# A graph-attention layer on one NeuronCore: batch 1's row flags by ScalarE, its x loaded later, value blocks cleared earlier

## The chip, the core and the metric

The kernel runs on one core of a Trainium2 chip. A core has a matrix engine (TensorE, PE in the profile, with PEld for its weight loads), VectorE (DVE), ScalarE (ACT), GpSimd (POOL), a queue processor for transfers (SyncE, SP) and 16 DMA engines between the chip's memory and the core's own (SBUF; PSUM receives the matrix products). Each engine works through its own instructions in order and waits on semaphores for the others. The metric is the device time of one execution in microseconds; lower is better.

## The reference

The layer gets x (16 batches, 512 nodes, 512 features), a condition vector per batch, and an integer adjacency (16, 512, 512, 11). Cut to what matters:

```python
row_zero = v.sum(-1) == 0                      # one flag for each node
q_exp = where(row_zero[..., None], 0.0, q[:, None, :])
self_feat = concat([v, q_exp], -1) @ W_self.T + b_self
output = self_feat
for d in range(2):                             # adjacency, and its transpose
    A = (adj if d == 0 else swap(adj))[:, :, :20, :]
    mask = A.sum(-1) > 0;  vb = A @ w_bias + b_bias
    kv = self_feat[:, :20]                     # 20 neighbours
    aff = (self_feat @ Wq[d].T + bq[d]) . (kv @ Wk[d].T + bk[d]) / sqrt(32)   # 16 heads
    w = softmax(where(mask, aff, -9e15) + vb)
    output += (w @ kv) @ Wout[d] + bout[d]     # by head
return v + relu(output)
```

A node whose features sum to zero gets no condition term. That flag for each node (the "row flag") is what the change computes in another way for batch 1.

## The kernel before

Everything is float32. There is a setup for all 16 batches together, and then a loop over the batches, in each of which four tiles of 128 nodes go through scores, softmax and weighted sum. The order of the instructions is written out by hand; no scheduler changes it. Tile pools decide which buffers are shared.

**Setup.** The 20 neighbours of all batches (320 columns) go through the self-feature product, the key product (`key_rows`) and, with Wq folded in, into keys ready for scores. `keys(runs)` works these out in 22 bursts of three half-batches each: matmuls into two PSUM pairs, then an eviction by ScalarE (one pair, L575) and VectorE (the other, L577) into a staging tile `st`, of which there are four. A staging tile is complete after four halves and goes out on SyncE's queue: the keys of batch 0 into `g0` (L582; the last four are copied by GpSimd, L584), those of batch 1 into the array `g1_d` (L585), those of batches 2 to 15 into `g_d` (L586, 1120 KB). Behind each burst stands filler work of TensorE, by `plan`: one word for each burst, one letter for each step ("b" biases, "c" bias scores, "v" and "w" values, "s" one step of batch 0's self features, "n" row flags of a batch). Extra work of other engines is hung on burst numbers (`if n == 10` and so on).

**Row flags.** For batches 0 and 1 GpSimd adds the four feature chunks of the transposed x (`row_sums`, three additions), and TensorE sums over the partitions with a matrix of ones (`row_flags`, L172), which also puts the sums on all partitions; VectorE compares with zero (L174). For batches 2 to 15 ScalarE sums rows of x in its natural layout (`row_sum`, L152, four passes for a batch on the tile `xn`), VectorE compares (`row_mask`, L156), SyncE stores 2 KB into `nz_d` (L157) and later loads it back on all partitions (`load_nz`, L161).

**Value blocks.** `blocks` puts projected values from `vw_d` into a block layout `bd_d` in memory (12 transfers, L145). What it doesn't write must be zero: `clear_blocks` writes zeros there for all batches (6 transfers, L129). `load_values` reads a batch's blocks (4 transfers, L117).

**The loop.** For batch b and tile nt, TensorE does the self-feature parts that `ahead` names (`self_feat`, L189), in tiles 0 and 1 the second half of batch b's nodes, in tile 3 the first half of batch b+1's, and then `scores` (L254). So batch 1's x is first read in tile 3 of batch 0. The weighted sums (`attend`, L321) of the batch before come in tile 2. VectorE evicts (`self_copy`, L202, which uses the row flags; `weigh`, L265 to L269), ScalarE takes exponentials, GpSimd normalises and adds masks. Transfers stand at fixed tiles: in tile 1 the next batch's adjacency half and `cq`, in tile 2 the value loads, keys, x two batches ahead and the other adjacency half. All of these go out on SyncE's queue in program order, and a transfer that has to wait holds those behind it.

Of the kernel before, what the change touches and what calls it, by code (L numbers as in the profile page):

```python
# [18 lines left out]
def gat_kernel(  # L19
# [53 lines left out]
    zero = const.tile([32, P], F32, name="zero")  # L73
# [12 lines left out]
    def load_x(b):  # L86
        xs[b] = load.tile([P, C, N], F32, tag="x", name=f"x{b}", bufs=4)
        nc.sync.dma_start(xs[b], xT[b].rearrange("(c p) n -> p c n", p=P))
# [74 lines left out]
    def row_sums(b):  # L163

        t = rss[b] = load.tile([P, 2, F], F32, tag="xn", name=f"rx{b}")[:, 0]
        nc.gpsimd.tensor_add(t, xs[b][:, 0], xs[b][:, 1])
        for k in range(2, C):
            nc.gpsimd.tensor_add(t, t, xs[b][:, k])
# [65 lines left out]
    def full_add(b, nt):  # L234
        f = fulls[b, nt] = msk.tile([P, H * S], F32, tag="full", name=f"full{b}_{nt}").rearrange(
            "p (g h m) -> p g h m", g=2, m=S
        )
        shape = [P, 2, H // 2, S]
        nc.gpsimd.tensor_add(  # L239
            f, cqs[b].unsqueeze(1).to_broadcast(shape),  # L240
            adds[b, nt // 2][:, nt % 2].unsqueeze(2).to_broadcast(shape),
        )
# [109 lines left out]
    with tc.tile_pool(name="setup", bufs=1) as sp:  # L352
# [18 lines left out]
        with tc.tile_pool(name="setup_k", bufs=1) as sk:  # L371
# [46 lines left out]
            nc.sync.dma_start(bo_sb, bout)  # L418
            for d in range(2):
                rows(wo_sb[:, d], woT[d])  # L420
            load_x(1)
            load_adj(0, 1)


# [80 lines left out]
        with tc.tile_pool(name="setup_g", bufs=4) as sg:  # L505
# [82 lines left out]
            def self_step(b, f, h, i, k):  # L588
# [5 lines left out]
            steps = {  # L594
                "b": [(biases, ())],
                "c": [(bias_scores, (d,)) for d in range(2)],
                "n": [(row_flags, (b,)) for b in range(2)],
                "s": [
                    (self_step, (0, f, h, i, k)) for f, h in ((0, 0), (1, 0), (0, 1))
                    for i in range(2) for k in range(C)  # L600
# [1 line left out]
                "v": [(values, (t, (d,), k)) for t in range(2) for d in range(2) for k in range(C)],  # L602
                "w": [(values, (2, (0, 1), k)) for k in range(C)],
            }
            plan = "bvv vv vv ccw vv ns ssss sssw vv vv ssss ssss vv vv nww ssss ssss".split()

            halves = [(fc, hg, d, i) for fc in range(C) for hg in range(C) for d in range(2) for i in range(2)]
            bursts = []
# [10 lines left out]
            for n, runs in enumerate(bursts):  # L619
                for i in range(len(rest)):  # L620
                    if i < (4 if n == 0 else 1) or any(fc == 0 and (d, hg) == rest[0] for fc, hg, d, _, _ in runs):
                        key_rows(*rest.pop(0))
                keys(runs)
                if rest:
                    for d in range(2):
                        bias_terms(d, n)
                    continue
                first = n if first is None else first
                for kind in plan[n - first] if n - first < len(plan) else ():
                    f, args = steps[kind].pop(0)  # L630
                    f(*args)
                if n == 7:
                    mask_count(0, 0)
                if n == 8:
                    mask_mul(0, 0)
                if n == 10:
                    mask_add(0, 0)
                    load_cq(0)
                if n == 11:
                    row_sums(1)  # L640
                if n == 12:
                    mask_count(0, 1)
                if n == 14:
                    mask_mul(0, 1)
                if n == 18:
                    full_add(0, 0)

    soft = ctx.enter_context(tc.tile_pool(name="soft", bufs=2))
    gp = ctx.enter_context(tc.tile_pool(name="gp", bufs=2))
# [2 lines left out]

    gs[0] = g0
    with tc.manual_schedule():
        load_keys(1)

        def side(t, lo, hi, q):

# [15 lines left out]
        for b in range(B):  # L674
# [13 lines left out]
            for nt in range(NT):  # L688
                store()
                if nt == 1:  # L690
                    if b + 1 < B:
                        load_adj(b + 1, 0)
                        load_cq(b + 1)
                    if b == 0:
                        clear_blocks(zero)
                        blocks()
                if nt == 2:
                    load_values(b)
# [78 lines left out]
                if nt < NT - 1:  # L777
                    if (b, nt + 1) not in fulls:
                        full_add(b, nt + 1)
                    if b == B - 1 and nt < 2:  # L780
                        ns = slice(nt * (N - P), N)
# [15 lines left out]
        b = B - 1  # L797
# [83 lines left out]
```

## Time and profile before

| | |
|---|---|
| three runs | 630.17, 630.88, 630.75 us (median 630.75) |
| the profiled execution | 630.1 us, of which the span in the trace is 627.1 us |
| granted TensorE clock | 1.00 |
| TensorE busy | 619.6 us |
| VectorE, GpSimd, ScalarE busy | 506.2, 342.1, 217.9 us |
| setup until batch 0's first scores | 91.65 us |
| one batch in the loop | some 33.3 us |

Timeline rows give the start and duration in us, the engine, the line, output<-input, how many instructions are merged, and in brackets the idle time before them and what ended it. "SPq" is SyncE issuing a transfer; its duration is that of the issue, not of the transfer. In rows by stretches each engine has its busy time and instruction count, in the order PE, PEld, DVE, ACT, POOL; the last three columns are the granted clock, the mean share in which the DMA engines were busy (packets overlap, so that it can be above 1), and GB/s.

### The profile page before, as it was taken

What the parts mean: (1) busy time and instruction counts of PE and PEld (TensorE: products, weight loads), DVE (VectorE), ACT (ScalarE), POOL (GpSimd) and SP (SyncE); (2) the same over time, 40 slices, a digit from 0 to 9 for tenths busy, and PEclk for the clock granted to TensorE, in tenths of its full rate; (3) what the DMA queues carried; (4) which work ended last, traced back from release to release, by engine and by line L of the source; (5) the groups of instructions that cost most, each with busy time, mean ns of one, the idle gap of its engine ahead of it and who ended that gap; (6) DMA issues with size and microseconds to landing.
All of it is one profiled execution on the core that took longest, in us unless ns stands there. A gap on an engine that the chain in (4) does not pass through costs nothing.

```text
span 627.1 us, 16412 instructions
## 1 busy us (share of the span) xinstructions
PE 619.6 (99%) x6830; PEld 380.3 (61%) x6830; DVE 506.2 (81%) x809; ACT 217.9 (35%) x480; POOL 342.1 (55%) x268
## 2 busy tenths in 40 slices
PE   8999999999999999999999999999999999999997
PEld 6654558866565656565565656565656565655654
DVE  1377657789888888888888979798888888888896
ACT  1445422133242424241524334332424242415341
POOL 2406332537556474738292847465564747382974
PEclk9999999999999999999999999999999999999999
DMA  8999998629284655738391919393757657492513
GB/s 303 399 393 320 360 389 247 219 76 304 102 251 154 188 219 120 286 97 310 56 350 33 334 45 290 112 289 116 232 174 186 220 135 271 87 320 49 184 36 135
DMA packets 88976, 131.53 MB, mean 210 GB/s; under 512 B 8808, under 2 KB 59016, under 8 KB 86856
## 3 DMA queue, kind: packets, MB, share of 16 engines
q1 hardware_dynamic: 87656, 128.61, 61.8%
q0 software_dynamic: 672, 1.36, 0.9%
q8 instruction: 53, 0.87, 0.6%
q10 hardware_dynamic: 576, 0.53, 0.3%
q14 instruction: 19, 0.16, 0.1%
HBM read 90.89 MB, written 39.92 MB: 209 GB/s over the span
## 4 chain that ended last, share of the span: by engine, by line
PE 97%; DMA 1%; issue 0%; SPq 0%; DVE 0%; ACT 0%; DVEq 0%
PE ps_s L254 44%; PE ps_sf L189 34%; PE ps_o L321 7%; PE ps_v L533 3%; PE ps_k L480 3%; DMA ws_q<-in_wsT 1%; PE ps_kv L431 1%; PE ps_o L667 1%; PE ps_nz L172 0%; PE ps_c L511 0%; PE ps_g(0, 3, 0, 0, 2)0_367 L560 0%; PE ps_q L441 0%; PE ps_g(1, 3, 1, 0, 2)0_530 L560 0%; PE ps_g(1, 1, 0, 1, 2)0_436 L560 0%; PE ps_g(3, 3, 0, 0, 2)0_799 L560 0%
## 5 line engine op out<-in xcount | busy, mean ns | idle before, releaser
L254 PE MATMUL ps_s<-g,sf 128*64 128x320 f32 x2048 | 287.5, 433 | 0.5 <-ACT st L575 0.5
L254 PEld LDWEIGHTS ps_s<-g,sf 128*64 128x64 f32 x2048 | 152.0, 137 | 119.9 <-issue 6.6
L189 PE MATMUL ps_sf<-x,ws_v 128*64 128x256 f32 (+1 forms) x2048 | 222.1, 371 | 0.0
L189 PEld LDWEIGHTS ps_sf<-x,ws_v 128*64 128x64 f32 x2048 | 151.5, 137 | 67.5 <-issue 2.6
L303 POOL TENSOR_TENSOR s<-s,sm 128x640 f32<-128x640 f32 x63 | 80.1, 1272 | 138.4 <-DVE sm L302 138.4
L274 ACT ACTIVATE s<-s 128x640 f32<-128x640 f32 x63 | 46.5, 738 | 214.4 <-DVE s L269 214.4
L239 POOL TENSOR_TENSOR full<-cq,both 128x640 f32<-128x640 f32 x64 | 99.0, 1547 | 25.2 <-ACT both L230 23.5
L211 POOL TENSOR_TENSOR prod<-prod,wb_sb 128x880 f32<-128x880 f32 x32 | 61.3, 1916 | 55.2 <-ACT prod L210 55.2
L265 DVE TENSOR_TENSOR ps_s<-ps_s,full 128x640 f32<-128x640 f32 x63 | 52.3, 830 | 38.6 <-PE ps_s L254 37.1
L343 POOL TENSOR_TENSOR o<-o,x 128x512 f32<-128x512 f32 x60 | 75.6, 1279 | 1.1 <-ACT o L340 1.1
L230 ACT COPY both<-add 64x80 f32<-64x80 f32 x128 | 32.8, 256 | 77.4 <-DVE add L225 76.3
L340 ACT ACTIVATE o<-o,bo 128x512 f32<-128x512 f32 x60 | 40.0, 714 | 44.3 <-DVE o L334 44.3
L301 DVE TENSOR_REDUCE sm<-s 128x32 f32<-128x640 f32 x63 | 51.6, 819 | 4.5 <-ACT s L274 0.9
L267 DVE TENSOR_REDUCE mx<-ps_s 128x32 f32<-128x640 f32 x63 | 52.0, 825 | 2.2
L269 DVE TENSOR_TENSOR s<-ps_s,mx 128x640 f32<-128x640 f32 x63 | 51.9, 824 | 2.2
L202 DVE SCALAR_TENSOR_TENSOR sf<-nz,qw,ps_sf 128x236 f32<-128x236 f32 (+1 forms) x128 | 52.6, 459 | 1.1 <-PE ps_sf L189 1.0
L310 DVE STREAM_TRANSPOSE wt<-s 128x640 f32<-128x640 f32 x63 | 52.6, 834 | 0.2 <-POOL s L303 0.2
L321 PE MATMUL ps_o<-wt,vd 32*32 32x256 f32 (+2 forms) x2176 | 45.8, 372 | 1.1 <-issue 1.1
L321 PEld LDWEIGHTS ps_o<-wt,vd 32*32 32x32 f32 x2176 | 30.2, 103 | 16.9 <-issue 8.5
L334 DVE TENSOR_TENSOR o<-ps_o,sf 128x512 f32<-128x512 f32 x60 | 36.3, 668 | 0.0
L152 ACT ACTIVATE xn<-xn 128x512 f32<-128x512 f32 x56 | 34.3, 613 | 0.0
L216 DVE TENSOR_REDUCE cond<-adj 128x80 f32<-128x880 int32 x32 | 33.2, 1037 | 1.2 <-DMA adj<-in_adj 1.2
(213 smaller groups left out, 423.1 us busy)
## 6 DMA issues: line engine op xcount, KB each, us to landing
g<-g_d SPq DMA_DIRECT2D x15, 1280.0 KB, 9.1
g_d<-st SPq DMA_DIRECT2D x16, 1120.0 KB, 6.4
x<-in_xT SPq DMA_DIRECT2D x16, 1024.0 KB, 11.0
out_T<-o SPq DMA_DIRECT2D x60, 256.0 KB, 4.3
xn<-in_xn SPq DMA_DIRECT2D x28, 512.0 KB, 8.5
adj<-in_adj SPq DMA_DIRECT2D x32, 440.0 KB, 7.2
vd<-bd_d SPq DMA_DIRECT2D x64, 128.0 KB, 4.0
nz<-nz_d SPq DMA_DIRECT2D x14, 256.0 KB, 4.9
```

Source lines behind the costliest of these rows:

```text
L189: nc.tensor.matmul(held[0][bass.ts(a, R), i * N // 2 : i * N // 2 + hi - lo], ws_v[:, k, bass.ds((2 * f + i) * P + a * R, R)], xs[b][:, k, ...
L202: nc.vector.scalar_tensor_tensor(sfs[b][:, 2 * f + i, lo:hi], nzs[b][:, lo:hi], qw[:, 2 * f + i, b : b + 1], ps[:, i * N // 2 : i * N // 2 ...
L211: nc.gpsimd.tensor_mul(p, p, wb_sb.unsqueeze(1).to_broadcast([P, 2 * S, L]))
L239: nc.gpsimd.tensor_add(f, cqs[b].unsqueeze(1).to_broadcast(shape), adds[b, nt // 2][:, nt % 2].unsqueeze(2).to_broadcast(shape),)
L254: nc.tensor.matmul(bank[bass.ts(a, R), : W // 2], sfs[b][:, k, bass.ds(nt * P + g * R, R)], keys[:, k, a], start=start and k == 0, stop=(k ...
L265: nc.vector.tensor_add(pw, pw, fulls.pop((b, nt)).rearrange("p g h m -> p g (h m)"))
L267: nc.vector.tensor_reduce(mx, p4, AX.X, ALU.max)
L269: nc.vector.tensor_sub(s, p4, mx.unsqueeze(3).to_broadcast(full))
L303: nc.gpsimd.tensor_mul(s, s, sm.unsqueeze(3).to_broadcast(full))
L310: nc.vector.transpose(wts[b][:, nt], s.rearrange("p a h m -> p (a h m)"))
L321: nc.tensor.matmul(banks[q][bass.ts(e, DH)].rearrange("p (t n) -> p t n", n=32), vds[b][r, e, i, q // 2 * 2 + n], wt[r, :, bass.ts(j, 32)] ...
L343: nc.gpsimd.tensor_add(o[:, c], o[:, c], xs[b][:, c])
```

## The change

- Batch 1's row flags are worked out as those of batches 2 to 15: its natural x is loaded (`load_xn`, two halves of 512 KB) behind bursts 10 and 12, ScalarE sums behind bursts 15 to 18, `row_mask(1)` stands behind burst 19, and the flags are loaded back in tile 1 of batch 0. `row_sums(1)` on GpSimd and `row_flags(1)` on TensorE go.
- `plan` has an "s" in the place of the second "n", so that batch 0's last self-feature steps are divided differently; their number stays 24.
- Batch 1's transposed x is no longer loaded among the setup's first loads but behind batch 1's keys, at the loop's start.
- The clears of the value blocks move from tile 1 of batch 0 to ahead of batch 1's keys.

```diff
@@ setup loads
                 rows(wo_sb[:, d], woT[d])
-            load_x(1)
             load_adj(0, 1)
@@ steps of the setup
-                "n": [(row_flags, (b,)) for b in range(2)],
+                "n": [(row_flags, (b,)) for b in range(1)],
...
-            plan = "bvv vv vv ccw vv ns ssss sssw vv vv ssss ssss vv vv nww ssss ssss".split()
+            plan = "bvv vv vv ccw vv ns ssss sssw vv vv ssss ssss vv vv sww ssss sss".split()
@@ behind the bursts
                 if n == 10:
                     mask_add(0, 0)
                     load_cq(0)
-                if n == 11:
-                    row_sums(1)
+                if n in (10, 12):
+                    load_xn(1, n // 2 - 5)
+                if 15 <= n < 19:
+                    row_sum(1, n - 15)
...
                 if n == 18:
                     full_add(0, 0)
+                if n == 19:
+                    row_mask(1)
@@ start of the loop
     with tc.manual_schedule():
+        clear_blocks(zero)
         load_keys(1)
+        load_x(1)
@@ tile 1 of batch 0
                     if b == 0:
-                        clear_blocks(zero)
+                        load_nz(1)
                         blocks()
```

## The prediction

> **What bounds the kernel now.** I read the share of each engine first, then the chain that ended last, then who TensorE waited for.
>
> ```profile
> span 627.1 us, 16412 instructions
> ...
> PE 619.6 (99%) x6830; PEld 380.3 (61%) x6830; DVE 506.2 (81%) x809; ACT 217.9 (35%) x480; POOL 342.1 (55%) x268
> ...
> PE 97%; DMA 1%; issue 0%; SPq 0%; DVE 0%; ACT 0%; DVEq 0%
> ```
>
> TensorE is busy for 619.6 of 627.1 us and carries 97% of the chain. In the whole run its listed waits are 1.1, 1.1, 0.6 and 0.5 us. So two things move the end: matmuls added or removed at their full length, and any new moment in which TensorE has nothing to do, also at full length, because nothing later has slack to give it back. All other engines count only as far as they make TensorE wait.
>
> Then I read the timeline of TensorE around the edits:
>
> ```profile
> 81.85 1.12 PE L172 MATMUL ps_nz<-rx,ones 128*128 128x512 f32 x2
> 82.91 1.94 PE L533 MATMUL ps_v<-wo_sb,kvT 128*64 128x512 f32 x8
> ...
> 91.65 4.60 PE L254 MATMUL ps_s<-g,sf 128*64 128x320 f32 x32 [0.52 <-ACT st L575]
> 96.01 3.69 PE L189 MATMUL ps_sf<-x,ws_v 128*64 128x256 f32 x32
> 99.46 8.85 PE L254 MATMUL ps_s<-g,sf 128*64 128x320 f32 x64
> 108.07 6.61 PE L189 MATMUL ps_sf<-x,ws_v 128*64 128x236 f32 x64
> ```
>
> The first row is the row-flag matmul of batch 1; the next matmul starts 1.06 us after it. The last row is the first use of batch 1's x: self_feat(1, ...) in tile 3 of batch 0, at 108.07. Then the queue of SyncE at the same place, where the moved transfers go:
>
> ```profile
> 92.03 0.32 SPq L586 DMA_DIRECT2D g_d<-st  x1
> 94.48 0.37 SPq L111 DMA_DIRECT2D g<-g_d  x1
> 94.91 2.27 SPq L96 DMA_DIRECT2D adj<-in_adj  x1
> 97.22 1.18 SPq L103 DMA_DIRECT2D cq<-cq_d  x2
> 98.44 6.12 SPq L129 DMA_DIRECT2D bd_d<-zero  x6
> 104.67 8.87 SPq L145 DMA_DIRECT2D bd_d<-vw_d  x12
> ```
>
> and the load of the DMA engines by stretches (the last two columns):
>
> ```profile
> 65.00:70.00 5.00, 5.00 (x32) 2.16 (x34) 3.81 (x7) 1.77 (x4) 0.09 (x1) 1.00 0.90 313
> 70.00:75.00 5.00, 5.00 (x64) 2.96 (x56) 2.67 (x5) 2.99 (x5) 2.51 (x2) 1.00 1.02 396
> 75.00:80.00 5.00, 5.00 (x41) 2.55 (x40) 2.98 (x6) 2.02 (x4) 0.32 (x1) 1.00 1.05 404
> 80.00:85.00 5.00, 5.00 (x33) 1.80 (x35) 2.92 (x6) 1.08 (x3) 0.89 (x2) 1.00 0.99 400
> 85.00:90.00 5.00, 5.00 (x60) 3.05 (x58) 2.89 (x5) 2.06 (x4) 2.88 (x4) 1.00 1.00 351
> 90.00:95.00 5.00, 4.48 (x39) 3.12 (x37) 1.41 (x4) 0.44 (x1) 1.87 (x2) 1.00 1.00 404
> 95.90:100.30 4.40, 4.40 (x43) 4.11 (x40) 2.99 (x4) 0.74 (x1) 0.00 (x0) 1.00 1.03 317
> ```
>
> From 70 us to the end of the setup the DMA engines are full, at about 400 GB/s, with the stores of key blocks. The last stretch is batch 1's key load: 317 GB/s over 4.4 us is its 1280 KB.
>
> **The change, part by part.** *The removed matmul.* TensorE loses one row-flag matmul: 82.91 - 81.85 = 1.06 us, at a granted clock of 1.00, all on the chain. The self_feat steps are regrouped (one moves into the gap of the removed "n"), their number stays 24. Gain 1.06 us; nothing else on TensorE shrinks. The uses that follow come 1.06 us earlier, so batch 1's x is wanted at 107.0.
>
> *GpSimd and VectorE.* Three additions of 1.3 us go off GpSimd (from 61.07), one 0.68 us comparison off VectorE, and a 0.17 us one comes. Nothing waited on them: counted as nothing.
>
> *ScalarE.* Four accumulating passes (613 ns, and the next starts 0.7 us later) stand behind the evictions of bursts 15 to 18. ScalarE idled 1.78, 1.85, 1.91 and 2.91 us ahead of the following evictions, so 0.7 us each is hidden. What could uncover them is a late xn: the eviction queued behind would hold the PSUM pair and TensorE. xn's first half is issued behind cq, near 65.3; at its median landing of 8.5 us it is there at 73.8, and ScalarE wants it at 74.3. With TensorE's filler behind each burst (1.94 us in the row at 82.91) I cost it at 0, at most 1.
>
> *The staging buffers.* Two xn halves (1024 KB) enter SyncE's queue at bursts 10 and 12, ahead of the key stores, which must land before their staging tile is written again, four tiles later. The store issued at 74.36 lands near 80.8 (median 6.4 us) and its tile is rewritten by the second eviction after 81.95, near 82.6: 1.8 us of margin. The delay worked out below uses that up, and the filler catches the rest: 0, at most 1.
>
> *Batch 1's x.* In the profile it is issued at 26.02 and is long there. Now it is the eighth transfer behind the last key store: six clears, batch 1's keys, then x, and the changed program makes SyncE hold x until that store, eight transfers back, has landed. Transfers of one queue land in order as far as landings tell (in a later batch keys after 9.1 us, x issued right behind them after 11.0). So what TensorE waits for is the sum of the bytes:
> - Last key store: issued 92.03, landing 5.2 us later, 97.2; its bytes are through at about 96.9.
> - Ahead of it there are now 1024 KB of xn: 1.05 MB at 404 GB/s, 2.6 us. What the queue left free between 65 and 95 absorbs part: shares of 0.90, 1.02, 1.05, 0.99, 1.00, 1.00 against 1.05 leave 0.34 x 5 = 1.7 us at most, 0.75 us if only the first stretch is truly free. 0.9 to 1.9 us stay; I take 1.6. The 1 MB taken out at 26 us does not help here, because the queue has free time again between 40 and 60 (shares of 0.89 and 0.96).
> - The clears: 2 x (192 + 128 + 64) = 768 KB in 512-byte pieces. Lower end: 0.79 MB at 404 GB/s, 1.9 us. Upper end: the 6.1 us in which SyncE issued them. The nearest row is that of the block copies, of the same pieces: between 108 and 114 us shares of 0.55 to 0.65 move 156 to 186 GB/s, so a full share is some 280 GB/s and 2.8 us. I take 3.4, near that row, with something of the way to the upper end, because these six are written from few SBUF partitions (24, 8 or 16).
> - Keys: 1.31 MB at 317 GB/s, 4.1 us. x: 1.05 MB at 404 GB/s, 2.6 us. From the last bytes to the landing some 0.8 us: x at 118.36 landed after 5.5 us, of which 512 KB ahead of it and its own bytes are 3.9, which leaves 1.6 for start and end together.
>
> Sum: 96.9 + 1.6 + 3.4 + 4.1 + 2.6 + 0.8 = 109.4. Wanted at 107.0: TensorE waits 2.4 us. The ends: 96.9 + 0.9 + 1.9 + 4.1 + 2.6 + 0.4 = 106.8, no wait; 96.9 + 1.9 + 6.1 + 4.1 + 2.6 + 1.0 = 112.6, a wait of 5.6. A check from a later batch: x issued at 177.15, right behind keys and 768 KB of other loads, landed after 11.0 us; issued at 98.5, when the last store has landed, that is 109.5.
>
> [...]
>
> *Behind x.* Batch 1's adjacency (440 KB, 1.1 us), cq and the new 256 KB flag load land after it, near 111.5 at the latest. VectorE wants the adjacency at 107.5 and is held some 3 us, with the maximum of tile 2 and the self_copy of batch 1 queued behind. TensorE needs that self_copy (116.06 to 117.6 today) at 122.21, and by then it is itself 1.3 us later: covered by more than 3 us. The next such point, the self_copy that ends at 135.5 and is wanted at 138.28, has 2.7. The block copies and the value loads keep their total issue time. Nothing counted; 0 to 1 if VectorE falls further back.
>
> Sum: -1.06 + 2.4 = +1.3 us. The profiled execution took 630.1 us (span 627.1 and 3.0 around it) and would take 631.4. The median of the runs, 630.75, is 0.65 above it, so the forecast is 632.1.
>
> **The rivals.** *x in time (not slower).* If the queue absorbs xn and the clears run at the full rate, x is there at about 107, and only the matmul counts: 630.75 - 1.06 = 629.7. It decides when x lands before 107.0, that is 2.4 us ahead of my sum. For it: clears wait for no data and can be moved in the 2 us in which SyncE stood still ahead of 94.48. Against it: those 2 us were idle for SyncE's queue only; the DMA engines were at a share of 1.00 and 404 GB/s.
>
> *A short wait.* A wait of 0.3 to 2.3 us, from any of the three estimates being 1 us too high, leaves -0.8 to +1.2: 630.0 to 632.0, no change that can be told.
>
> *The setup stalls.* xn late or a staging tile not free: evictions late, TensorE waits up to 1 us twice in the setup, and x comes no earlier. With a wait for x of 2.4 that is 633 to 634. Against it: the margins above.
>
> **How the numbers follow.** 0.2% is 1.26 us, about what a measurement of this kernel can tell from no change. A wait for x of over 2.3 us: 0.45; a short wait: 0.30; x in time: 0.18; a setup stall on top: 0.07. Slower: 0.45 + 0.07 = 0.52. Faster by over 1.26 us needs more than the matmul gives; about half of the case of x in time could be measured there: 0.09. Within: 0.39. The range goes from x in time, 629.7, to a wait of 4.6 with the clears near their upper end, 630.75 - 1.06 + 4.6 = 634.3; the likeliest case alone reaches from 632.0 to 634.3.
>
> **What would show it.** In the waits of TensorE a new row "L189 waits for DMA x", of about 2.4 us, near 107 in the timeline; 1.1 us less of L172; SyncE's x issued near 98 and landing near 109. No such row means that the first rival holds; waits of L560 for ScalarE or VectorE mean the third. The prediction is wrong if key stores end before 97 in spite of xn, or if the clears take 2 us.

## The result: slower by 1.1%, five microseconds more than predicted

| | before | after |
|---|---|---|
| median of four runs each | 630.82 us (630.17 to 630.94) | 636.88 us (636.39 to 637.93) |
| ratio | 1 | 1.0107, 95% interval 1.0092 to 1.0122 |
| the profiled execution, and its span | 630.1 us, 627.1 us | 636.39 us, 633.8 us |
| mean granted TensorE clock | 1.00 | 0.995 |

The direction was right, the size was not: +6.06 us where +1.3 was forecast, outside the range. The page of the kernel after, in the lines that answer to those of before (span, TensorE's share, the chain that ended last):

```profile
span 633.8 us, 16418 instructions
...
PE 620.7 (98%) x6828; PEld 373.8 (59%) x6828; DVE 505.8 (80%) x809; ACT 221.0 (35%) x488; POOL 337.8 (53%) x265
...
PE 97%; DMA 2%; SPq 0%; DVE 0%; issue 0%; ACT 0%; DVEq 0%
```

TensorE still carries the chain, and the chain's DMA share has gone from 1% to 2%. TensorE's waits name the transfer:

```profile
PE ps_sf L189 <- DMA x<-in_xT: 7.2, 1, 7.2
```

One wait of 7.2 us, where the prediction had 2.4. TensorE's timeline around it (before, its last rows began at 99.46 and 108.07):

```profile
90.00 4.60 PE L254 MATMUL ps_s<-g,sf 128*64 128x320 f32 x32 [0.45 <-ACT st L574]
...
113.87 8.96 PE L189 MATMUL ps_sf<-x,ws_v 128*64 128x236 f32 x64 [7.21 <-DMA x<-in_xT]
122.67 4.47 PE L254 MATMUL ps_s<-g,sf 128*64 128x320 f32 x32
...
142.59 2.75 PE L321 MATMUL ps_o<-wt,vd 32*32 32x256 f32 x128
145.28 4.53 PE L254 MATMUL ps_s<-g,sf 128*64 128x320 f32 x32
```

Three things are to be seen. The row that waited is also longer: 8.96 us for the 64 matmuls that took 6.61 before. The first row, with which the loop's work begins, starts 1.65 us earlier than before (90.00 against 91.65). And the weighted sums of batch 0 (L321) run in one piece of 2.75 us, which they didn't do before: there, six of them ran and 122 came later. These rows of the kernel before, which the prediction did not show, become important below:

```profile
134.44 0.63 PE L321 MATMUL ps_o<-wt,vd 32*32 32x256 f32 x6
135.66 2.70 PE L321 MATMUL ps_o<-wt,vd 32*32 32x256 f32 x122 [0.58 <-issue]
```

TensorE's longer row has its reason in the clock. The stretches of after, with the granted clock in the third column from the end:

```profile
106.00:113.80 7.80, 0.66 (x6) 0.10 (x2) 0.99 (x2) 0.00 (x0) 1.27 (x1) 0.88 1.06 358
113.80:122.70 8.90, 8.83 (x66) 5.77 (x68) 7.51 (x9) 1.81 (x3) 3.46 (x3) 0.72 0.53 153
122.70:131.00 8.30, 8.30 (x72) 4.77 (x70) 6.32 (x11) 1.77 (x5) 3.20 (x4) 1.00 0.87 279
```

A mean clock of 0.88 over 7.8 us and 0.72 over 8.9 us make 1.9 and 5.0 us at half the clock. The trace's clock records have it as one stage of 6.83 us at 0.5 that begins at 111.88, which is 5.2 us after TensorE's last matmul had ended (106.66), and goes on for some five microseconds after work had come back. The prediction had no term for it.

SyncE's queue in after shows why x was late:

```profile
88.10 1.69 SPq L157 DMA_DIRECT2D nz_d<-nz  x1
89.89 2.19 SPq L584 DMA_DIRECT2D g_d<-st  x1
92.19 1.44 SPq L585 DMA_DIRECT2D g_d<-st  x1
93.68 8.41 SPq L129 DMA_DIRECT2D bd_d<-zero  x6
102.20 1.03 SPq L111 DMA_DIRECT2D g<-g_d  x1
103.27 2.80 SPq L88 DMA_DIRECT2D x<-in_xT  x1
106.12 2.12 SPq L96 DMA_DIRECT2D adj<-in_adj  x1
```

The two stores of keys took 0.32 us each to issue at this place in before; here the first takes 2.19 and the second 1.44, behind the flags' own store with 1.69. The clears took 8.41 us to issue in place of 6.12. By the trace's landings the last key store is through at 100.17 (before 97.24), the keys are there at 111.02 and x at 113.83.

**Where the microseconds lie.** The start of a run varies (TensorE's wait for the weights `ws_q` near 10 us is between nothing and 2.1 us in the kernels of this study), so I count from the start of the loop's first score row (91.65 before, 90.00 after). Each later point is the start of a TensorE row of the profiles:

| from the loop's first scores to | before | after | difference |
|---|---|---|---|
| first use of batch 1's x (L189) | 16.42 | 23.87 | +7.45 |
| the scores behind it (L254) | 22.80 | 32.67 | +9.87 |
| the scores behind batch 0's weighted sums | 46.63 | 55.28 | +8.65 |
| the end of the span | 535.45 | 543.80 | +8.35 |

So the wait makes 7.45, the half clock another 2.42; 1.22 come back at the weighted sums; and from there to the end, nearly 490 us, only 0.3 us more come back. Of the 1.65 us at the start, 0.92 are the removed matmul (from the second group of the neighbours' self-feature matmuls, which starts at 11.43 and 10.70, to the first scores it is 80.22 us before, 79.30 after), the rest is the start of the run. 8.35 - 1.65 = 6.7, the difference of the spans.

### The profile page after: what moved, and what is told of

It reads as the page before. It is cut to its first block, busy times and chain, and to the rows that moved or that the text cites. A ratio compares the mean times of both kernels' runs of the same rounds, so it can differ in the third digit from the quotient of the medians.

```text
span 633.8 us, 16418 instructions
## 1 busy us (share of the span) xinstructions
PE 620.7 (98%) x6828; PEld 373.8 (59%) x6828; DVE 505.8 (80%) x809; ACT 221.0 (35%) x488; POOL 337.8 (53%) x265
## 4 chain that ended last, share of the span: by engine, by line
PE 97%; DMA 2%; SPq 0%; DVE 0%; issue 0%; ACT 0%; DVEq 0%
PE ps_s L254 43%; PE ps_sf L189 34%; PE ps_o L321 7%; PE ps_v L532 3%; PE ps_k L479 3%; DMA x<-in_xT 2%; PE ps_kv L430 2%; PE ps_o L672 1%; PE ps_warm L390 1%; PE ps_c L510 0%; PE ps_g(0, 3, 0, 0, 2)0_365 L559 0%; PE ps_nz L172 0%; PE ps_q L440 0%; PE ps_g(3, 0, 0, 0, 2)0_700 L559 0%; PE ps_g(1, 2, 0, 0, 2)0_478 L559 0%; PE ps_g(1, 1, 0, 1, 2)0_434 L559 0%
## 5 line engine op out<-in xcount | busy, mean ns | idle before, releaser
L254 PE MATMUL ps_s<-g,sf 128*64 128x320 f32 x2048 | 287.3, 433 | 0.5 <-ACT st L574 0.5
L189 PE MATMUL ps_sf<-x,ws_v 128*64 128x256 f32 (+1 forms) x2048 | 224.5, 374 | 7.2 <-DMA x<-in_xT 7.2
L254 PEld LDWEIGHTS ps_s<-g,sf 128*64 128x64 f32 x2048 | 148.7, 137 | 123.1 <-issue 6.6
L189 PEld LDWEIGHTS ps_sf<-x,ws_v 128*64 128x64 f32 x2048 | 148.4, 138 | 80.3 <-DMA x<-in_xT 7.8
L202 DVE SCALAR_TENSOR_TENSOR sf<-nz,qw,ps_sf 128x236 f32<-128x236 f32 (+1 forms) x128 | 52.6, 459 | 0.7 <-PE ps_sf L189 0.7
L310 DVE STREAM_TRANSPOSE wt<-s 128x640 f32<-128x640 f32 x63 | 52.6, 834 | 0.2 <-POOL s L303 0.2
L321 PE MATMUL ps_o<-wt,vd 32*32 32x256 f32 (+2 forms) x2176 | 45.3, 372 | 0.4 <-issue 0.4
L216 DVE TENSOR_REDUCE cond<-adj 128x80 f32<-128x880 int32 x32 | 33.2, 1037 | 8.0 <-DMA adj<-in_adj 8.0
L321 PEld LDWEIGHTS ps_o<-wt,vd 32*32 32x32 f32 x2176 | 30.0, 103 | 15.9 <-issue 7.9
L152 ACT ACTIVATE xn<-xn 128x512 f32<-128x512 f32 x60 | 36.8, 614 | 0.0
```

Source lines behind the costliest of these rows:

```text
L189: nc.tensor.matmul(held[0][bass.ts(a, R), i * N // 2 : i * N // 2 + hi - lo], ws_v[:, k, bass.ds((2 * f + i) * P + a * R, R)], xs[b][:, k, ...
L202: nc.vector.scalar_tensor_tensor(sfs[b][:, 2 * f + i, lo:hi], nzs[b][:, lo:hi], qw[:, 2 * f + i, b : b + 1], ps[:, i * N // 2 : i * N // 2 ...
L254: nc.tensor.matmul(bank[bass.ts(a, R), : W // 2], sfs[b][:, k, bass.ds(nt * P + g * R, R)], keys[:, k, a], start=start and k == 0, stop=(k ...
L310: nc.vector.transpose(wts[b][:, nt], s.rearrange("p a h m -> p (a h m)"))
L321: nc.tensor.matmul(banks[q][bass.ts(e, DH)].rearrange("p (t n) -> p t n", n=32), vds[b][r, e, i, q // 2 * 2 + n], wt[r, :, bass.ts(j, 32)] ...
```

## The experiments

The theory of the prediction was that one transfer, x, decides, and that VectorE's late inputs behind it are covered by about 3 us. The first runs take x's wait apart. Every ratio is to runs of the kernel before made beside that kernel: their median was 631.11 us for the first four experiments, 631.07 for the next four and 630.41 for the last four.

**x back in the setup.**

```diff
@@ setup loads
                 rows(wo_sb[:, d], woT[d])
+            load_x(1)
             load_adj(0, 1)
@@ start of the loop
         load_keys(1)
-        load_x(1)
```

> The changed kernel with one part undone: batch 1's x is loaded among the setup's first loads again. Theory (the loss is TensorE's wait for this x and the low clock behind it): no row of L189 waiting for x, the granted clock 1.00 throughout, and 1.06 us under the kernel before, about 629.7 us (629.2 to 630.4). Rival (ScalarE's four passes, the xn loads or the late adjacency cost time in the setup or in batch 0): over 632 us with waits of TensorE for ScalarE, VectorE or the adjacency's followers.

Measured: 636.58 us, ratio to before 1.0082 (1.0061 to 1.0103). The wait for x is gone and nothing is gained. TensorE loses the time elsewhere:

```profile
129.79 4.50 PE L254 MATMUL ps_s<-g,sf 128*64 128x320 f32 x32
136.66 0.70 PE L321 MATMUL ps_o<-wt,vd 32*32 32x256 f32 x6 [2.37 <-DVE wt L310]
140.26 4.46 PE L321 MATMUL ps_o<-wt,vd 32*32 32x256 f32 x122 [2.90 <-issue]
144.65 4.90 PE L254 MATMUL ps_s<-g,sf 128*64 128x320 f32 x32
```

It stands twice in the weighted sums of batch 0, for 2.37 and 2.90 us, and then 122 matmuls take 4.46 us where they took 2.70: the lower clock again (0.994 in the mean of the span). VectorE in the same run:

```profile
112.52 1.07 DVE L216 TENSOR_REDUCE cond<-adj 128x80 f32<-128x880 int32 x1 [4.51 <-DMA adj<-in_adj]
...
129.58 1.07 DVE L216 TENSOR_REDUCE cond<-adj 128x80 f32<-128x880 int32 x1 [2.03 <-DMA adj<-in_adj]
...
139.30 0.86 DVE L202 SCALAR_TENSOR_TENSOR sf<-nz,qw,ps_sf 128x256 f32<-128x256 f32 x2
```

VectorE waits 4.51 and 2.03 us for the two halves of batch 1's adjacency (L216 counts its masks), and everything behind on VectorE moves back. The weighted sums need two things from VectorE: the transposed weights (L310), and four PSUM banks, the last of which is free when `self_copy` (L202) has emptied it. That instruction ends at 140.16, and TensorE goes on at 140.26. The wait that the profile calls "issue" is this one.

Here the theory of the prediction falls, and a second one takes its place, which the expectations below call that of the late queue: **SyncE's list runs several microseconds late at the loop's start, whatever stands in it is late, and there are two consumers, TensorE for x and VectorE for the adjacency; either one alone costs the whole, since VectorE has no slack to the weighted sums.** In the kernel before, the same `self_copy` ended at 135.55 and TensorE went on at 135.66: no slack was left there either, and it had already cost 1.2 us. VectorE's rows of the kernel before, the second half of the adjacency and that `self_copy`:

```profile
124.97 1.07 DVE L216 TENSOR_REDUCE cond<-adj 128x80 f32<-128x880 int32 x1 [1.25 <-DMA adj<-in_adj]
...
134.69 0.86 DVE L202 SCALAR_TENSOR_TENSOR sf<-nz,qw,ps_sf 128x256 f32<-128x256 f32 x2
```

**Clears back in tile 1, x behind the keys.**

```diff
@@ start of the loop
-        clear_blocks(zero)
         load_keys(1)
         load_x(1)
@@ tile 1 of batch 0
                         load_nz(1)
+                        clear_blocks(zero)
                         blocks()
```

> The changed kernel with the clears put back into tile 1 of batch 0, x still behind batch 1's keys. Theory (the clears, which took 8.4 us to issue while the DMA engines were half busy, are what makes x late): x is issued near 99 and lands near 107.5, TensorE waits 0 to 1.5 us and keeps its clock, 629.7 to 631.5 us. Rival (the bytes of xn, stores and keys ahead of x are enough): x still lands at 110 or later, TensorE waits over 3 us, over 633 us.

Measured: 637.85 us, ratio 1.0106 (1.0064 to 1.0149). x came at 106.78 and TensorE waited only 0.49 us for it, so most of its delay had been the six clears: counted from the loop's first scores it landed 17.1 us later in place of 23.8. The time went to the weighted sums: waits of 4.26 us for the weights and 2.48 us for the banks. VectorE's timeline has the reason:

```profile
130.44 1.07 DVE L216 TENSOR_REDUCE cond<-adj 128x80 f32<-128x880 int32 x1 [7.10 <-DMA adj<-in_adj]
```

The second half of the adjacency is issued behind clears, blocks and value loads, at 124.10, and VectorE stands 7.10 us for it (1.25 us before).

**x ahead of clears and keys.**

```diff
@@ start of the loop
+        load_x(1)
         clear_blocks(zero)
         load_keys(1)
-        load_x(1)
```

> The changed kernel with x ahead of the clears and of batch 1's keys. Theory (x only has to be ahead of the clears): x lands near 103, no wait, about 629.7 us (629.2 to 630.6); VectorE and ScalarE then wait some 3 us for batch 1's adjacency, near 107, at no cost. Rival (whatever comes late behind the clears holds TensorE next: adjacency, keys or flags): over 632 us, with a wait of TensorE behind 110 us.

Measured: 637.89 us, ratio 1.0107 (1.0065 to 1.0149). x is there at 103.51, TensorE has no wait for it; VectorE waits 6.36 us for the first half of the adjacency,

```profile
114.66 1.07 DVE L216 TENSOR_REDUCE cond<-adj 128x80 f32<-128x880 int32 x1 [6.36 <-DMA adj<-in_adj]
```

and TensorE stands 1.13 and 2.91 us in the weighted sums and 2.07 us ahead of a score row at 124.14. The same total by a third way.

**The clock kept up.** Twelve spare passes of matmuls stand in the wait for x.

```diff
@@ loop, ahead of self_feat
+                if (b, nt) == (0, NT - 1):
+                    spare = ps_acc.tile([P, 512], F32, tag="acc", name="ps_spare")
+                    for _ in range(6):
+                        nc.tensor.matmul(spare, ws_v[:, 0, :P], xs[0][:, 0], start=True, stop=True)
```

> The changed kernel with six matmuls more, each two passes of 128x512 and some 1.06 us, into a spare PSUM bank that nobody reads, right ahead of the first use of batch 1's x; they only fill the wait of 7.2 us. Theory (2.4 us of the loss is the half clock that TensorE is granted after 5 us without work): the granted clock stays at 1.00, the row of 8.96 us for the first self features of batch 1 is back at about 6.6, and the time falls by 2.4 us to about 634.5 (634.0 to 635.2). Rival (the longer row is something else, as slow reads of x beside the DMA traffic): the row stays near 9 us, and the time at 636.9 or above.

Measured: 638.63 us, ratio 1.0116 (1.0071 to 1.0161). TensorE's timeline:

```profile
108.67 5.42 PE L730 MATMUL ps_spare<-x,ws_v 128*128 128x512 f32 x12
115.95 6.59 PE L189 MATMUL ps_sf<-x,ws_v 128*64 128x236 f32 x64 [1.86 <-DMA x<-in_xT]
...
142.30 0.63 PE L321 MATMUL ps_o<-wt,vd 32*32 32x256 f32 x6
145.66 4.03 PE L321 MATMUL ps_o<-wt,vd 32*32 32x256 f32 x122 [2.73 <-issue]
```

The row behind the wait is back at 6.59 us: the clock's part of the reason, 2.4 us, is shown. But the time is not gained. TensorE reaches the weighted sums earlier and stands there for VectorE, 2.73 us, with the clock falling after it (4.03 us for 122 matmuls that took 2.70, a mean clock of 0.997 over the span). The spare matmuls take a bank of the same pool, so part of that wait may be theirs.

The next runs were chosen to separate the two theories: by the second, x and the adjacency have to be early together, and then the whole loss goes.

**x and both adjacency halves ahead of the clears.** It differs from the run with x alone ahead in two loads.

```diff
@@ start of the loop
+        load_x(1)
+        load_adj(1, 0)
+        load_adj(1, 1)
         clear_blocks(zero)
         load_keys(1)
-        load_x(1)
@@ tile 1
-                        load_adj(b + 1, 0)
+                        if b > 0:
+                            load_adj(b + 1, 0)
@@ tile 2
-                    if b + 1 < B:
+                    if 0 < b < B - 1:
                         load_adj(b + 1, 1)
```

> Edit: the changed kernel with batch 1's x and then both halves of its adjacency ahead of the clears at the loop's start; flags by ScalarE, clears ahead of the keys and all else as changed. The run x_first differs only in the two adjacency loads. Theory of the late queue (SyncE's list at the loop's start runs late, and VectorE, which has no slack there, waits for the adjacency; its lateness reaches TensorE by the banks and the transposed weights of attend): x lands by 104, the halves by about 109, wanted at 108.3 and about 124; the 6.4 us that VectorE waited in x_first go, and attend in batch 1's tile 2 starts without a wait or with one under 1 us: 629.0 to 631. Theory of the prediction (only x matters): as x_first, 637.9. Rival (the clears and stores are slow on the DMA engines, and whatever comes behind them is late): the keys, the row flags or the value blocks take the adjacency's place, 633 to 637.

Measured: 628.19 us, ratio 0.9948 (0.9934 to 0.9963): faster than the kernel before. Moving two transfers of 440 KB is worth 9.7 us against 637.89. VectorE's and TensorE's rows:

```profile
108.80 1.01 DVE L216 TENSOR_REDUCE cond<-adj 128x80 f32<-128x880 int32 x1
117.55 1.57 DVE L202 SCALAR_TENSOR_TENSOR sf<-nz,qw,ps_sf 128x236 f32<-128x236 f32 x4 [1.20 <-DMA nz<-nz_d]
...
123.84 1.01 DVE L216 TENSOR_REDUCE cond<-adj 128x80 f32<-128x880 int32 x1
```

```profile
134.65 2.75 PE L321 MATMUL ps_o<-wt,vd 32*32 32x256 f32 x128
```

Both mask counts start without a wait, the 128 matmuls run in one piece, and the mean granted clock of the span is 1.00. The clears, the keys, the flags and the blocks are as late as ever in this run (keys at 116.40, flags later); TensorE didn't wait for any of them. That excludes the rival in which the next transfer in the list would take the adjacency's place.

**The kernel before with its second adjacency half early.**

```diff
@@ before.py, tile 1
                         load_adj(b + 1, 0)
+                        if b == 0:
+                            load_adj(1, 1)
@@ tile 2
-                    if b + 1 < B:
+                    if 0 < b < B - 1:
                         load_adj(b + 1, 1)
```

> Edit: the kernel before with the second half of batch 1's adjacency loaded right behind the first, in batch 0's tile 1, in place of tile 2. Theory of the late queue: VectorE's 1.25 us wait for this half at 124.97 goes, and with it the 1.2 us that TensorE lost in attend at 134.44 (self_copy ends at 135.55 there, 122 matmuls start at 135.66): 629.3 to 630.2, span 626.0. Theory that VectorE had 2.7 us to spare there, as the prediction held: no change, 630.8. Rival: the value blocks behind it are 1 to 2 us later and attend waits for them: 631 to 633.

Measured: 629.26 us, ratio 0.9972 (0.9961 to 0.9984). The weighted sums begin without a break,

```profile
134.28 2.75 PE L321 MATMUL ps_o<-wt,vd 32*32 32x256 f32 x128
136.96 4.53 PE L254 MATMUL ps_s<-g,sf 128*64 128x320 f32 x32
```

and the row behind them starts 45.48 us after the loop's first scores in place of 46.63: 1.15 us gained, by a load that the prediction held to have 2.7 us to spare. This is the plainest proof that VectorE had no slack.

**The clears' move alone, in the kernel before.**

```diff
@@ before.py, start of the loop
+        clear_blocks(zero)
         load_keys(1)
@@ tile 1 of batch 0
                     if b == 0:
-                        clear_blocks(zero)
                         blocks()
```

> Edit: the kernel before with only the clears moved ahead of batch 1's keys; flags by TensorE, x in the setup. Theory of the late queue: no more is issued ahead of the blocks than before, so they and the second adjacency half come when they came; the first half is issued about 101 and lands about 109 against 108.6 wanted, a wait of 0 to 2 us for VectorE: 630.8 to 633. If the move of the clears carries the loss: 635 to 637. Theory of the prediction: 630.8.

Measured: 633.84 us, ratio 1.0035 (1.0020 to 1.0050). In the profiled execution (631.7 us) the loop has lost nothing, on the contrary. TensorE's timeline:

```profile
137.22 3.05 PE L321 MATMUL ps_o<-wt,vd 32*32 32x256 f32 x128
140.20 4.53 PE L254 MATMUL ps_s<-g,sf 128*64 128x320 f32 x32
```

The last row starts 45.77 us after the loop's first scores (94.43), 0.86 us less than before, and to the end of the span it is 534.57 against 535.45. Of the 2.78 us by which its loop starts later than before's, 2.1 lie in the first 20 us: a wait of 2.06 us for the weights `ws_q`, and a stage of 3.41 us at half the clock behind it (a mean of 0.91 over the first 20 us), in which eight self-feature matmuls of the neighbours take 3.40 us where they take 2.39. The edit doesn't touch that part of the program. Why its median is 2.8 us above that of before is left open: the profiled execution is 2.1 us below that median. Six of the ten executions took 633.7 to 634.9 us at mean clocks of 0.995 to 0.997, and the profiled one isn't among them, so a further stage at half the clock in those six is possible and not shown. In the profiled one VectorE's wait for the first adjacency half was 1.89 us and for the second 0.26, and none of it reached TensorE.

**The flags by ScalarE alone.** x is back in the setup and the clears in tile 1.

```diff
@@ setup loads
+            load_x(1)
             load_adj(0, 1)
@@ start of the loop
-        clear_blocks(zero)
         load_keys(1)
-        load_x(1)
@@ tile 1 of batch 0
                         load_nz(1)
+                        clear_blocks(zero)
                         blocks()
```

> Edit: the changed kernel with x back in the setup and the clears back in tile 1, so that only the row flags by ScalarE, with their xn loads, store and read back, are left of the change. Theory of the late queue: the 1 MB of xn puts the last key store back by 2 to 3 us, the keys' load waits for it at the head of SyncE's list, so blocks and second adjacency half are 3 to 4 us late (landing about 128 to 129 against 124.95), and VectorE waits 4 to 5 us for it: 633 to 636. Theory of the prediction (xn costs the queue 1.6 us, no engine waits for what is behind): 629.7, the row-flag matmul saved. If the clears carry the loss: 629.7 too.

Measured: 637.81 us, ratio 1.0102 (1.0082 to 1.0122). So the flags alone cost as much as the whole change, without any wait for x. The keys' load on SyncE's queue, then VectorE's and TensorE's timelines:

```profile
100.45 0.37 SPq L111 DMA_DIRECT2D g<-g_d  x1
```

```profile
132.02 1.07 DVE L216 TENSOR_REDUCE cond<-adj 128x80 f32<-128x880 int32 x1 [6.54 <-DMA adj<-in_adj]
```

```profile
139.09 0.70 PE L321 MATMUL ps_o<-wt,vd 32*32 32x256 f32 x6 [2.83 <-DVE wt L310]
142.69 4.47 PE L321 MATMUL ps_o<-wt,vd 32*32 32x256 f32 x122 [2.90 <-issue]
```

The keys' load is issued at 100.45 (94.48 before; 1.75 us of the difference are the later start of this run's loop, with its first scores at 93.40), since SyncE holds it until earlier stores have landed; the last key store lands 9.22 us after the loop's first scores, 5.59 before. Then the second adjacency half is late by 5.3 us on the same scale, and VectorE and TensorE follow. The time is above the 633 to 636 expected because VectorE waits 6.54 us where 4 to 5 were expected, and because the half clock comes on top (122 matmuls in 4.47 us, a mean clock of 0.992 over the span), which that expectation left out.

The last runs fill the table of the two loads, measure two terms of the prediction's sum, and try an order that is better still.

**x late, the second adjacency half early.**

```diff
@@ after.py, tile 1
                         load_adj(b + 1, 0)
+                        if b == 0:
+                            load_adj(1, 1)
@@ tile 2
-                    if b + 1 < B:
+                    if 0 < b < B - 1:
                         load_adj(b + 1, 1)
```

> Edit: the changed kernel with the second half of batch 1's adjacency loaded right behind the first, in tile 1; x stays behind clears and keys. With x_early (x in time, adjacency late: 636.6) and x_adj_first (both in time: 628.2) this makes the fourth field: adjacency in time as far as VectorE is held up anyway, x late. Theory of two late loads, each of which costs the whole by itself: TensorE still waits about 7 us for x and has about 2.4 us of half clock, VectorE has no wait for the second half: 635.5 to 637. If the adjacency alone carried the loss: 629 to 631.

Measured: 636.94 us, ratio 1.0109 (1.0093 to 1.0124), as the second theory has it. TensorE's timeline:

```profile
115.19 9.35 PE L189 MATMUL ps_sf<-x,ws_v 128*64 128x236 f32 x64 [6.78 <-DMA x<-in_xT]
...
144.30 2.76 PE L321 MATMUL ps_o<-wt,vd 32*32 32x256 f32 x128
```

| | adjacency late | adjacency early |
|---|---|---|
| x late | 636.88 (the change) | 636.94 (second half only) |
| x early | 636.58 (x in the setup), 637.89 (x first in the loop) | 628.19 |

Neither load alone gives anything; both together give 9 us. In the field at the upper right the first half is still late, but VectorE's wait for it (8.10 us, to 116.87) lies for the most part inside TensorE's wait for x. A kernel with x late and both halves early was not run.

**The flags without their 1 MB of loads.** Batch 1's rows are set to one and not read, so its flags don't come from the input.

```diff
@@ load_xn
         t = xns[b, h] = load.tile([P, 2, F], F32, tag="xn", name=f"xn{b}_{h}")
+        if b == 1:
+            nc.gpsimd.memset(t, 1.0)
+            return
```

> Edit: the changed kernel with batch 1's rows for the flags not loaded from memory but set to one by POOL, so that its 1 MB is off SyncE's queue; ScalarE's sums, the flags' store and their read back stay. The flags of batch 1 are then not computed from the input. Prediction's price of that load for the queue: 1.6 us. By flags_only, where the last key store landed 102.6 against 97.2, it is 3.5 to 4.5 us. Then x lands at 109.5 to 110.5 in place of 113.8, TensorE waits 3 to 4 us and its clock stays up: 631.5 to 634. By 1.6 us: a wait of 5.6 us, at the edge of the half clock, 634 to 636.

Measured: 636.13 us, ratio 1.0088 (1.0070 to 1.0105), above the 631.5 to 634 of the higher price and at the upper end of the 634 to 636 that the prediction's price gave. TensorE's timeline:

```profile
113.04 9.05 PE L192 MATMUL ps_sf<-x,ws_v 128*64 128x236 f32 x64 [5.21 <-DMA x<-in_xT]
```

The wait is 5.21 us in place of 7.21, so the load's price for x is 2.0 us: the prediction's 1.6 was nearly right, and my 3.5 to 4.5 was wrong. The last key store lands 7.89 us after the first scores, with the load 10.17, before 5.59. The other 2.3 us come without those bytes: the flags' store takes 1.91 us to issue here too, and the key stores next to it 1.1 to 1.6. That the 2 KB store itself makes the queue slow is not shown: the key store issued ahead of it, at 87.56, already took 1.59 us, where the same store took 0.45 in before. And the clock still fell, for 6.83 us (a mean of 0.54 from 111 to 114 us and of 0.77 from 114 to 123), though the wait was only 5.21 us: the row is 9.05 us long. From the first scores to the end of the span it is 542.2 us in place of 543.8, so 1.6 of the 2.0 us reach the end in these two profiles; the ratios of the medians, 1.0088 and 1.0107, overlap in their intervals and don't tell them apart.

**One wide clear.** All 2 MB of the blocks are written by one transfer from 128 partitions, in pieces of 1 KB, in place of six transfers of 0.79 MB in all.

```diff
@@ clear_blocks
-        for e in range(HL):
...
+        to = bd_d.rearrange("b r e i c g -> (b r) (e i c g)").rearrange("(p q) (a w) -> p (q a) w", q=4, a=HL)
+        nc.sync.dma_start(to, zero.unsqueeze(1).to_broadcast([P, 4 * HL, 2 * P]))
```

> Edit: the changed kernel with the six clears of 0.79 MB in pieces of 512 bytes replaced by one DMA that clears all 2 MB of the blocks in pieces of 1 KB from 128 partitions. If the price of the clears lies in their issue and in the uneven use of the DMA engines (share of 0.4 to 0.7 while they run): one issue of 1 to 3 us in place of 8.4, share above 0.9, x issued about 98 and landing 108 to 112, TensorE's wait 2 to 5 us: 631 to 635. If it lies in the bytes: 2 MB take 5 to 6 us on top of the keys, x lands at 113 or later, 636 to 639.

Measured: 637.14 us, ratio 1.0111 (1.0098 to 1.0124). A stretch of the DMA engines' load, and TensorE's timeline:

```profile
97.00:104.00 7.00, 7.00 (x61) 5.01 (x58) 5.71 (x9) 1.74 (x5) 1.27 (x1) 1.00 1.02 364
```

```profile
113.12 8.28 PE L181 MATMUL ps_sf<-x,ws_v 128*64 128x236 f32 x64 [4.38 <-DMA x<-in_xT]
```

The transfer's part was as expected: one issue of 1.11 us, the DMA engines full at 364 GB/s (in after 175 GB/s at a share of 0.69 between 97 and 106), and 5.3 us from the last key store's landing to its own for 2 MB, where six clears of 0.79 MB cost 5.7 to 7.0 (below). The wait for x fell to 4.38, inside the 2 to 5 expected. The time did not follow: the clock fell for 3.41 us in spite of the shorter wait (a mean of 0.90 from 111 to 114 us and of 0.84 from 114 to 123; the row takes 8.28 us against 6.6), VectorE waited 1.70 us for the second adjacency half, and TensorE stood again in the weighted sums. The 631 to 635 failed for the same reason as above: I priced a wait and not what it sets off.

**The loads first, the clears back in tile 1.**

```diff
@@ against the kernel with x and both halves ahead of the clears
         load_adj(1, 1)
-        clear_blocks(zero)
         load_keys(1)
@@ tile 1 of batch 0
                         load_nz(1)
+                        clear_blocks(zero)
                         blocks()
```

> Edit: x_adj_first with the clears back in tile 1, behind the row flags' load; x, both adjacency halves and the keys are ahead of all else at the loop's start. Theory of the late queue: the row flags, for which VectorE waited 1.2 us at 117.55 in x_adj_first, come some 8 us earlier; the value blocks come when they came. TensorE's 0.9 us in attend goes: 627.2 to 628.2. Rival (clears behind make blocks and attend's values late): 629 to 632.

Measured: 628.43 us, ratio 0.9967 (0.9954 to 0.9981), not to be told from the 628.19 above (0.9948, 0.9934 to 0.9963). VectorE's timeline at batch 1's `self_copy`:

```profile
115.90 1.56 DVE L202 SCALAR_TENSOR_TENSOR sf<-nz,qw,ps_sf 128x236 f32<-128x236 f32 x4
```

VectorE's wait for the flags has gone, as expected, and was worth nothing that can be measured. The 0.9 us of TensorE that the expectation meant to gain are still there (0.89 at 622.00 in the kernel with x and both halves ahead of the clears, 0.93 at 621.69 here): that wait stands in the weighted sums at the very end of the program, not in those of batch 0. Where the clears stand doesn't matter once x and the adjacency are ahead of them.

## Why the prediction was right or wrong, by its steps

Two steps failed in the measured time: the wait for x was sized at 2.4 us and was 7.2, and the slower clock behind a wait was put at nothing without a reason and was worth 2.4 us. A third, the slack of VectorE, was wrong too and would have cost as much with x in time.

- **"Any new moment in which TensorE has nothing to do counts at full length, because nothing later has slack to give it back."** Right from batch 1's third tile on. Ahead of it 1.22 of 9.87 us came back, which the kernel before had itself lost there. In after, the loss at that tile, 8.65 us, is still 8.35 at the end; in the kernels of the experiments the two differ by 0.4 us at most.
- **The removed matmul, -1.06 us.** 0.92 in after. In five of the other kernels with the flags on ScalarE half of it is lost again: TensorE waits 0.4 to 0.5 us at L559 for ScalarE's eviction. This is what the prediction bounded as 0 to 1.
- **"1024 KB of xn: I take 1.6."** 2.0 by the run without the load. Left out was what the rest of the flags' move does to the queue, with the flags' own store and the slow issue of the key stores next to it: another 2.3 us on the last key store. Counted from the loop's first scores, the sum had that store's end at 98.5 - 90.6 = 7.9; it was 10.2.
- **"Clears: I take 3.4."** Mis-sized. From the last key store to batch 1's keys it is 10.85 us in after; the keys alone take 3.86 (in the kernel before with the early adjacency half, 97.11 to 100.97) or 5.20 (with the flags alone, 102.62 to 107.82). So the clears cost 5.7 to 7.0 us, about the upper end of 6.1 that I had read from their issue time, which was itself 8.4 here; with the clears back in tile 1, x landed 6.7 us earlier. (The stretch from which the keys' price was read, 317 GB/s over 4.4 us, is 1.39 MB, so it holds more than the keys' 1.31.) The one wide clear moves 2.7 times the bytes in 5.3 us. That the few partitions make the six slow was my estimate; the wide clear differs in partitions, pieces and number of transfers at once and does not tell these apart.
- **Wait for x of 2.4 us, upper end 5.6.** 7.2. The terms above make it: +2.3 for stores, +3.35 for clears and keys together, -0.6 for x and its tail, -0.25 for the time at which it was wanted.
- **A wait costs its length.** This step was silent and wrong: 7.2 us of standing still brought 6.83 us of half clock, worth 2.4 us. The prediction's own upper end, 5.6 us, was long enough for it (5.21 was), even 2.4 was no safe length (waits of 2.06 and 2.00 us in the setup of two kernels had 3.41 us of half clock behind them), and a slower clock appears nowhere in the text.
- **"The next such point, the self_copy that ends at 135.5 and is wanted at 138.28, has 2.7."** Wrong, and the step that would have sunk the forecast even with x in time. It was wanted at 135.5: the weighted sums wait for its bank, and the row shown above, 122 matmuls that start at 135.66 behind six at 134.44, said so in the profile before. I took the next score row as the point of need, and passed over the 0.58 us listed as "issue". There was no margin: TensorE already stood for that instruction in the kernel before, and went on 0.1 us after its end. VectorE was also held longer than the "some 3 us" of this step, 7.98 us in after; the earlier self_copy, "covered by more than 3 us", was so in after, but with x ahead of the clears TensorE stood 2.07 us until 124.14, just after it had begun (123.60).
- **The rival "x in time", 629.7.** Falls as it was put. With x in time the kernel took 636.58. What reaches the rival's side is x and adjacency in time, 628.19.
- **"A setup stall on top."** Not seen in after, and in the other kernels not beyond the 0.4 to 0.5 us above.

## What to carry to other kernels

When a step is moved in a queue, list everyone who reads what stands behind it, and find for each the instruction of the bounding engine that needs it, by buffers as well as by data: an accumulation bank that another engine must first empty is such a need, and two rows of one line with a gap between them show it. Two late inputs with nearly the same delay hide each other, so that putting one right shows nothing; put both right before concluding that the queue isn't the cause. And a wait of some microseconds on TensorE is to be priced with the slower clock behind it (2.4 us behind 7.2 us here), not by its length alone.

## What the runs showed of the hardware that I had not expected

- The granted clock fell to 0.5 in stages of 3.41, 6.83 and 10.24 us, multiples of one length. The waits of TensorE in front of them were 4.38 us (3.41 at half clock), 5.21 and 7.21 (6.83), and 6.78 (10.24). Shorter ones had a lower clock behind them as well: two of 2.37 and 2.90 with six matmuls between them (122 matmuls in 4.46 us in place of 2.70), one of 2.73 in the run with the spare matmuls (122 in 4.03), and in the setup one of 2.06 (the clears alone) and one of 2.00 (the flags alone), with 3.41 us at half clock each (a mean of 0.91 over the first 20 us in both). One of 1.81 in the setup of the wide clear had none: the mean clock of its span, 0.996, has no room for a second stage. The clock fell 5.2, 3.4, 4.7 and 2.2 us after TensorE's last matmul (in the change, the run without the 1 MB, the wide clear and the late x with the early adjacency half), so that 5.2 us is one value of several. In the kernel before, without such a wait, the clock records have 1.00 from 6.08 us to the end of the span.
- What may order these values is a grid in time. In the traces of before and after every change of the clock lies a whole number of 3.413 us behind its first rise, which comes 6.08 and 6.07 us after the span's start: in after the fall 31 of them (105.81 us) and the rise 33, the next fall 184, in before the only fall 182. In after, the stretch from 105.06 to 108.47 had 1.60 of 3.41 us busy and the clock stayed, the next had none and it fell at 111.88, the next had 1.43 and it stayed low, the next was full and it rose at 118.71. Up to 600 us all other such stretches of the two traces were busy for 82% or more, and the clock stayed at 1.00 behind each. This is read from two traces, and no run was made to test it; that the price of a wait depends on where it falls in the grid is an estimate from them. Its length alone does not give it: 6.78 us had 10.24 us of half clock behind it, 7.21 had 6.83.
- The time to issue a transfer on SyncE is no constant: the same key store took 0.32 us in before and up to 2.19 us in after, the six clears between 5.57 and 8.87 us in these kernels. Whether a full queue or the transfers themselves set it was not tried.
- Six clears of 0.79 MB in pieces of 512 bytes from few partitions held the queue for 5.7 to 7.0 us at a DMA share of 0.69, while one of 2 MB in pieces of 1 KB from 128 partitions took 5.3 us at a share of 1.02.
